# Token transposes of the last part: from TensorE passes to VectorE block transposes and on-chip transfers

## The chip, the cores and the metric

The kernel runs on one core of one Trainium2 chip. The metric is the device time of one execution in microseconds. Before the change three runs gave 5923.83 (the median), 5930.9 and 5917.58 us.

## What is computed

The input is x, 32 images of 128 channels by 64 x 64 pixels, f32. Cut to what matters:

```python
x = x + conv(group_norm(x), weight, butterfly matrices)   # in a transform domain, 64 x 64 per image
t = x.reshape(32, 128, 4096).transpose(0, 2, 1)           # tokens: 4096 x 128 per image
n = layer_norm(t)
k, v = n @ Wk.T + bk, n @ Wv.T + bv
probs = softmax(einsum('sbe,sbf->sef', k, v) / sqrt(32))
t = t + einsum('sef,sbf->sbe', probs, n)
n = layer_norm(t)
p = softmax(n @ router_w + router_b); the two best experts of 8, their p scaled to sum 1
t = t + sum over the two of p_e * (n @ expert_w[e] + expert_b[e])
out = t.transpose(0, 2, 1)
```

In the attention each image has its own 128 x 128 matrix of scores over channels; the sum runs over that image's 4096 tokens. The outer `x` after the convolution is called x1 below: it lies with channels on the 128 partitions, and attention and experts want tokens there.

## The kernel before

The kernel has three parts, one after the other. The first normalizes each image and transforms it (to about 940 us), the second multiplies by the convolution's weights for each of 64 columns (to about 2560 us). Both are untouched. The third part (`transfers`, `conv`, `front` and `experts`, from L800 on) takes image after image through these stages. An image has 32 tiles of 128 tokens, handled as 8 groups of four.

- `conv`: inverse transform by TensorE (`pu` L910, `py` L933; for images 0 and 1 in smaller pieces, `pw` L961 and `pz` L982), ScalarE copies between, and VectorE's sum with the image `y` (L942, op `ho`), which leaves x1 in a tile `x1_b` of 16 x 2 x 4 x 32 elements per partition.
- `front`, op `pt` (L1066): four TensorE transposes of 128 x 128 bring a group of x1 to tokens in PSUM. Op `to` (L1071): ScalarE copies the group into the token tile `tk` of this image (two tiles in turn, [128, 32, 128], so image b shares its tile with image b-2). Op `sa` (L1035, L1037): VectorE takes the statistics of four token tiles.
- then `pwa` and `na` (a power on ScalarE, a Newton step on GpSimd), `xg` (L1101, ScalarE: normalized tokens), `pg` (L1112, TensorE: Gram matrix), the small softmax chain (`gs`, `pb`, `t1`, `sm`, `pr`, `pc`, `prx`), `pp` (L1185, TensorE: x1 times the folded attention matrix and router), `at` (L1196, ScalarE), `ad` (L1211 to L1213 and statistics, VectorE: adds into `tk`), and the choice of experts (`l2` to `gt`, VectorE).
- `experts`: `xn` (L1300, ScalarE), `px` (L1310, TensorE transposes), `xT` (L1316, ScalarE), `pe` (L1323, TensorE: 64 products of 128 x 512 per image into three PSUM buffers), `m` (L1334, VectorE: product times gate, into `tm`), `s` (L1359 to L1362, GpSimd: sums over experts, into `tk`), `so` (L1368, VectorE: stream transposes of 32 x 32 blocks into `so`), `os` (L1378, SP: four stores per group).

What sets the order: every op is added to a `Plan` with engine, estimated time, due time, and the ops it comes after. The third part does not use the planner's own order. A table `ORDER`, written out by hand, lists all ops of one image with a stage (0 to 4); an op of image b stands at b + stage + its place in the table, and small shifts in `EDGE` move ops of images 0, 1, 30 and 31. `follow` issues them in that order, so each engine's queue is fixed: five images are in flight, and an engine that waits for one op holds all ops behind it. SP's queue holds the loads `r` (two per op) and `y` and the stores `os`. `room` counts buffers: 3 PSUM tiles for `pe`, 2 (`tl`) for `pt`, `px`, `pp` and the softmax chain, 8 rings for `r`, 4 `xg`, 2 each of `xn`, `tm`, `so`.

Of the kernel before, what the change touches and what calls it, by code (L numbers as in the profile page):

```python
# [10 lines left out]
F32 = mybir.dt.float32  # L11
# [92 lines left out]
def kernel(  # L104
# [732 lines left out]
    kvb = kc.tile([P, 2, P], F32, name="kvb")  # L837
    nc.gpsimd.dma_start(kvb[:, 0, :], bk.partition_broadcast(P))
    nc.gpsimd.dma_start(kvb[:, 1, :], bv.partition_broadcast(P))
    u = up.tile([P, n, P], F32, name="u")  # L840
    tk = [ct.tile([P, NT, P], F32, name=f"tk{i}") for i in range(2)]
    xg = [ct.tile([P, 4, P], F32, name=f"xg{i}") for i in range(NG)]
# [26 lines left out]
    plan = Plan({"cv": 1, "pe": 3, "tl": 2, "r": 8, "xg": NG, "xn": 2, "tm": 2, "so": 2})  # L869
# [157 lines left out]
    def front(b):  # L1027

        t = tk[b % 2]
        v = {}  # L1030

        def bn(which, lo, hi):
            bs = st.tile([P, 4, 6], F32, name=f"bs{which}_{b}_{lo}", tag="bs", bufs=2)
            for i in range(lo, hi):
                nc.vector.bn_stats(bs[:, i - lo, :], t[:, i, :])  # L1035
            for i in range(lo, hi):
                nc.vector.bn_aggr(v["mv", which][:, i, :], bs[:, i - lo, :])  # L1037
# [22 lines left out]
        def turn(g):  # L1060
            def run():
                ps = tile_of["pt", b, g] = tps.tile([P, 512], F32, tag="tl", name=f"pt{b}_{g}")
                x1 = ys[b].rearrange("c l v a w -> c (l v a w)")
                for k in range(4):
                    i = 4 * g + k
                    nc.tensor.transpose(ps[:, k * P : (k + 1) * P], x1[:, i * P : (i + 1) * P], ident)  # L1066
            return run

        def turned(g):
            def run():  # L1070
                nc.scalar.copy(  # L1071
                    t[:, 4 * g : 4 * g + 4, :].rearrange("p k c -> p (k c)"), tile_of.pop(("pt", b, g))
                )
            return run
# [10 lines left out]
        for g in range(8):  # L1085
            at = s1 + 0.016 * g
            add(b, f"pt{g}", "PE", 0.48, at, turn(g), [(b - 2, f"so{g}")] + [f"ho{k}" for k in range(4)], ("tl",))
            add(b, f"to{g}", "ACT", 0.55, at, turned(g), [f"pt{g}"], (), ("tl",))
            add(b, f"sa{g}", "DVE", 0.85, at, stats1(g), [f"to{g}"] + (["sa0"] if g else []))
# [6 lines left out]
        def norm(g):  # L1096
            def run():
                rstd, nmr, above = (v[1][:, k, :] for k in range(3))
                for k in range(4):
                    i = 4 * g + k  # L1100
                    nc.scalar.activation(  # L1101
                        xg[g % NG][:, k, :], t[:, i, :], AF.Identity, bias=above[:, i : i + 1], scale=rstd[:, i : i + 1]
                    )
            return run

        def gram(g):
            def run():
                if g == 0:
                    v["pg"] = tps.tile([P, 512], F32, tag="tl", name=f"pg{b}")
                for k in range(4):  # L1110
                    i = 4 * g + k
                    nc.tensor.matmul(  # L1112
                        v["pg"][:, 0:P], xg[g % NG][:, k, :], xg[g % NG][:, k, :],
# [4 lines left out]
        for g in range(8):  # L1118
            at = s1 + 0.26 + 0.016 * g
            add(b, f"xg{g}", "ACT", 1.65, at, norm(g), ["na", (b if g >= NG else b - 1, f"pg{(g - NG) % 8}")], ("xg",))  # L1120
# [85 lines left out]
        def added(lo, m):  # L1206
            def run():
# [3 lines left out]
                nc.vector.tensor_tensor(t[:, lo : lo + m, :], ps[:, :, 0:P], t[:, lo : lo + m, :], ALU.add)  # L1211
# [79 lines left out]
    def experts(b):  # L1291
        t = tk[b % 2]

        def normal(g):
            def run():
                rstd, nmr = tile_of["norm", b]
                x = tile_of["xn", b, g] = wp.tile([P, 4, P], F32, tag="xn", name=f"xn{b}_{g}")
                for k in range(4):
                    i = 4 * g + k
                    nc.scalar.activation(  # L1300
                        x[:, k, :], t[:, i, :], AF.Identity, bias=nmr[:, i : i + 1], scale=rstd[:, i : i + 1]
# [39 lines left out]
        def weighed(i, half):  # L1341

            def run():
                ps = tile_of.pop(("pe", b, i, half))
                for e in range(4):
                    nc.vector.scalar_tensor_tensor(  # L1346
                        t[:, i, :], ps[:, e * P : (e + 1) * P], tile_of["gate", b][:, i, 4 * half + e : 4 * half + e + 1],
                        t[:, i, :], ALU.mult, ALU.add,
# [6 lines left out]
        def summed(j):  # L1355
            def run():
# [4 lines left out]
                for m in range(2):  # L1361
                    nc.gpsimd.tensor_tensor(t[:, lo : lo + 2, :], t[:, lo : lo + 2, :], tm[:, :, m, :], ALU.add)  # L1362
            return run

        def flip(g):
            def run():
# [3 lines left out]
                    in_=t[:, 4 * g : 4 * g + 4, :].rearrange("p t (k c) -> p t k c", c=32),  # L1370
# [44 lines left out]
    for b in range(B):  # L1415
# [5 lines left out]
        s1:4 px2:4 m4_0:4 pe5_0:4 xT2:4 m5_1:4 pwa:3 pe6_0:4 ho0:2 px3:4 pe4_1:4 h1:2 m4_1:4 xn6:4 m5_0:4 na:3  # L1421
        m6_0:4 pe6_1:4 ho1:2 s2:4 xg0:3 pe7_1:4 pe7_0:4 m7_0:4 m6_1:4 h2:2 xT3:4 so0:4 xg2:3 xg1:3 m7_1:4 pe8_0:4
        ho2:2 pe9_0:4 s3:4 m8_0:4 xg3:3 pe8_1:4 m9_0:4 pg0:3 m8_1:4 pg1:3 pe9_1:4 xg5:3 pe10_1:4 pe10_0:4 m9_1:4
        xg4:3 pe11_0:4 s4:4 m10_0:4 pg2:3 so1:4 pg3:3 xg6:3 os1:4 xg7:3 pg4:3 pe11_1:4 xn5:4 pg5:3 m11_1:4 m11_0:4
        pg6:3 r1:1 m10_1:4 pg7:3 s5:4 pe12_0:4 gs:3 pe13_1:4 m12_0:4 pb:3 pe12_1:4 t1:3 pe13_0:4 os0:4 r2:0 pb2:3
        h3:2 sm:3 m13_0:4 pr:3 xT4:4 sr:3 m12_1:4 sn:3 m13_1:4 pe14_0:4 s6:4 m14_0:4 pc:3 pe15_1:4 pe15_0:4 prx:3
        ho3:2 pp0:3 m15_0:4 px5:4 at0:3 pe14_1:4 m15_1:4 pe19_0:4 m14_1:4 xT5:4 ad0:3 pe18_0:4 xn7:4 s7:4 pp6:3
        m18_0:4 pe19_1:4 at6:3 pp9:3 w0:1 m19_0:4 m19_1:4 at9:3 ad6:3 pe18_1:4 r7:1 wo0_0:1 ad9:3 pe16_0:4 wo0_1:1
        pp21:3 m18_1:4 pe16_1:4 at21:3 m16_0:4 so3:4 s9:4 pp12:3 m16_1:4 w1:1 at12:3 ad21:3 r4:0 x:1 os3:4 pe17_1:4
        wo1_0:1 ad12:3 pe17_0:4 wo1_1:1 pp24:3 m17_1:4 pe22_0:4 m17_0:4 at24:3 s8:4 pp3:3 m22_0:4 w2:1 at3:3 ad24:3  # L1430
        pe23_0:4 ad3:3 wo2_0:1 pe22_1:4 wo2_1:1 pp30:3 m22_1:4 pe23_1:4 m23_0:4 at30:3 pp15:3 m23_1:4 w3:1 ad30:3
        at15:3 s11:4 so4:4 pe21_1:4 ad15:3 wo3_0:1 r5:0 os4:4 px6:4 pe20_0:4 wo3_1:1 pe20_1:4 m20_0:4 xT6:4 pp18:3
        m20_1:4 pe21_0:4 m21_1:4 at18:3 pp27:3 m21_0:4 w4:1 at27:3 s10:4 ad18:3 pe26_0:4 ad27:3 wo4_0:1 pe27_1:4
        pe26_1:4 m26_0:4 pwb:3 m27_1:4 pt0:2 so2:4 pe24_0:4 m26_1:4 pe27_0:4 m24_0:4 pt1:2 m27_0:4 to0:2 nb:3
        pe25_1:4 to1:2 so5:4 wo4_1:1 pe25_0:4 m25_1:4 os5:4 s13:4 px7:4 m25_0:4 pe24_1:4 xT7:4 l2:3 xn0:3 pt2:2 f1:3
        w5:1 f2:3 pt5:2 pe30_0:4 m24_1:4 wo5_0:1 f3:3 pe31_0:4 wo5_1:1 s12:4 pe30_1:4 m30_0:4 to2:2 to5:2 w6:1 sa0:2
        m31_0:4 m30_1:4 pe31_1:4 pt4:2 m31_1:4 pt3:2 to4:2 f4:3 pe28_1:4 px0:3 pe29_1:4 sa5:2 wo6_0:1 s15:4 sa4:2
        wo6_1:1 sa1:2 pe28_0:4 w7:1 xn1:3 f5:3 xT0:3 to3:2 m28_0:4 so6:4 m28_1:4 m29_1:4 os6:4 pe29_0:4 xn4:3 pt6:2
        m29_0:4 px1:3 gt:3 pe0_0:3 s14:4 to6:2 pe1_1:3 m0_0:3 r6:0 os2:4 pe0_1:3 m1_1:3 wo7_0:1 pe1_0:3 pe3_0:3
        px4:3 wo7_1:1 sa6:2 m1_0:3 m0_1:3 pe2_0:3 xn3:3 xn2:3 xT1:3 sa2:2 s0:3 pe3_1:3 m2_0:3 h0:1 m3_1:3 so7:4  # L1440
        m3_0:3 sa3:2 os7:4 pe2_1:3 pt7:2 r0:0 r3:0 pe4_0:3 pe5_1:3 m2_1:3 to7:2 sa7:2
# [3 lines left out]
            at:-0.001152 f:0.024239 gs:-0.002876 gt:0.000645 h:-0.088197 ho:-0.107173 l:-0.011950 m:-0.001978  # L1445
            na:-0.062269 nb:0.023962 os:0.037831 pb:-0.003357 pc:0.004368 pe:-0.004859 pg:-0.007392
            prep:-0.061921 prx:-0.000723 pt:-0.339605 pwa:-0.154931 pwb:0.037324 px:0.004889 r:-0.551854
            s:-0.000175 sa:-0.148905 sm:-0.006267 sn:0.000807 so:-0.001240 sr:0.003296 t:-0.002368 to:-0.321139
            w:-0.120521 wo:-0.109642 x:0.001867 xT:0.001275 xg:0.001692 xn:0.024691
        """,  # L1450
        1: """
            ad:0.003202 at:0.005763 f:0.005458 gs:-0.006322 gt:-0.000499 h:0.054990 ho:0.051746 l:-0.039944
            m:-0.001956 na:-0.011054 nb:-0.006237 os:0.010755 pc:-0.007414 pe:-0.000758 pg:0.001613 pr:-0.004399
            prx:-0.010090 pt:-0.015523 pwa:0.002034 pwb:0.001095 px:-0.002083 r:0.003449 s:-0.001956 sa:0.014227
            sn:-0.012403 so:-0.008148 sr:-0.010178 t:0.008140 to:0.002048 w:-0.000799 wo:-0.000193 xT:-0.009151
            xg:0.001343 xn:0.009969
        """,
        B - 2: """
            ad:-0.000137 at:0.005214 f:0.009800 gt:0.013838 h:-0.001798 ho:-0.002170 l:0.001614 m:0.011670
            na:0.002329 nb:-0.000549 os:0.199427 pb:-0.000148 pc:-0.004225 pe:0.008786 pg:-0.022172 pp:-0.005288  # L1460
            pr:-0.000058 prx:-0.004077 pt:-0.004342 pwa:-0.000635 pwb:-0.005281 px:0.016961 r:-0.007120
            s:0.049524 sa:-0.000213 sm:0.000159 sn:0.010880 so:0.176068 sr:0.012703 t:0.003951 w:0.001356
            wo:-0.009915 x:0.098978 xT:0.012789 xg:0.005833 xn:0.039799
        """,
        B - 1: """
            ad:0.016785 at:0.025250 f:0.011554 gt:0.005035 h:0.014633 ho:-0.003864 m:0.001746 na:0.022282
            nb:0.003897 os:0.161384 pb:-0.000741 pc:-0.008894 pe:0.004175 pg:0.007134 pp:0.006191 pr:-0.001474
# [75 lines left out]
```

## Time and profile before

| | |
|---|---|
| profiled execution | 5924.1 us, span of the core 5922.4 us |
| granted TensorE clock, mean | 0.993 |
| busy of the span: TensorE, VectorE, ScalarE, GpSimd | 98%, 72%, 65%, 67% |
| third part begins, first expert product | about 2560 us, 2679.4 us |
| `pt`, TensorE, in 3500 to 5500 us | 612 rows, mean 273 ns |
| `to`, ScalarE copy of 128x512 | 153 rows, mean 584 ns |
| `so`, VectorE stream transpose of 128x512 | 156 rows, mean 704 ns |
| stores `os` on SP, 64 KB | 1024, median 434 ns of SP each |
| loads `r` on SP, 256 KB | 496, median 589 ns of SP each |
| DMA | 756.88 MB, mean 128 GB/s |

How to read it: a busy row is the union of an engine's instructions. TensorE's instructions overlap, so the mean of a matmul row is longer than its share of the queue. Rows named SPq are times in which SP issued a transfer, not the transfer. In a line of groups the numbers behind the bar are busy us and mean ns of one, and behind the second bar the idle time just before, with what ended it. Some matmul rows are missing from the record (612 of about 628 here).

### The profile page before, as it was taken

What the parts mean: (1) busy time and instruction counts of PE and PEld (TensorE: products, weight loads), DVE (VectorE), ACT (ScalarE), POOL (GpSimd) and SP (SyncE); (2) the same over time, 40 slices, a digit from 0 to 9 for tenths busy, and PEclk for the clock granted to TensorE, in tenths of its full rate; (3) what the DMA queues carried; (4) which work ended last, traced back from release to release, by engine and by line L of the source; (5) the groups of instructions that cost most, each with busy time, mean ns of one, the idle gap of its engine ahead of it and who ended that gap; (6) DMA issues with size and microseconds to landing.
All of it is one profiled execution on the core that took longest, in us unless ns stands there. A gap on an engine that the chain in (4) does not pass through costs nothing. (4 is left out here: it accounts for less than half of the span.)

```text
span 5922.4 us, 221064 instructions
## 1 busy us (share of the span) xinstructions
PE 5789.1 (98%) x94348; PEld 4560.4 (77%) x94348; DVE 4235.4 (72%) x10353; ACT 3837.7 (65%) x7089; POOL 3947.6 (67%) x4210
## 2 busy tenths in 40 slices
PE   7999999999999999979999999999999999999997
PEld 7999999999999999976666666666666666666653
DVE  5565555555555555538888878788888888787877
ACT  7666664555555555557777777777777777777762
POOL 2110006666666666607888888888888888888887
PEclk9999999999999999989999999999999999999999
DMA  5767766666666666652323222233223222222201
GB/s 194 241 228 233 236 210 206 171 174 171 171 173 173 172 172 173 158 159 61 97 76 87 79 79 87 82 88 83 88 75 97 76 84 81 79 86 83 77 21 29
DMA packets 664681, 756.88 MB, mean 128 GB/s; under 512 B 70608, under 2 KB 462288, under 8 KB 659600
## 3 DMA queue, kind: packets, MB, share of 16 engines
q1 hardware_dynamic: 661088, 733.69, 43.0%
q8 instruction: 740, 12.12, 0.9%
q0 software_dynamic: 2608, 9.06, 0.5%
q14 instruction: 245, 2.01, 0.1%
HBM read 406.79 MB, written 335.54 MB: 125 GB/s over the span
## 5 line engine op out<-in xcount | busy, mean ns | idle before, releaser
L1323 PE MATMUL pe<-ew_sb,xT 128*128 128x512 f32 x4096 | 1973.2, 600 | 36.6 <-DVE tm L1334 22.8
L1334 DVE TENSOR_TENSOR tm<-pe,oh 128x512 f32<-128x512 f32 x2028 | 1298.4, 678 | 369.1 <-PE pe L1323 259.4
L1359 POOL TENSOR_TENSOR tm<-tm 128x512 f32<-128x512 f32 x1014 | 1270.4, 1272 | 287.0 <-DVE tm L1334 282.2
L1323 PEld LDWEIGHTS pe<-ew_sb,xT 128*128 128x128 f32 x4096 | 691.8, 190 | 552.1 <-issue 325.3
L660 DVE COPY f<-g 128x1024 f32<-128x1024 f32 x508 | 622.4, 1225 | 651.9 <-PE g L649 651.9
L671 PE MATMUL m<-f,s 128*64 128x64 f32 x32768 | 1071.3, 224 | 1.7 <-ACT f L660 0.8
L671 PEld LDWEIGHTS m<-f,s 128*64 128x64 f32 x32768 | 1001.1, 138 | 63.2 <-issue 2.5
L617 POOL COPY s<-l 128x512 f32<-128x512 f32 x512 | 546.2, 1102 | 527.3 <-issue 510.4
L660 ACT COPY f<-g 128x1024 f32<-128x1024 f32 x508 | 514.9, 1014 | 562.4 <-PE g L649 536.3
L1362 POOL TENSOR_TENSOR tk<-tk,tm 128x256 f32<-128x256 f32 x1014 | 737.9, 728 | 79.5
L1360 POOL TENSOR_TENSOR tm<-tm 128x512 f32<-128x512 f32 x507 | 644.7, 1272 | 39.8
L649 PE MATMUL g<-c,wst 9*128 9x128 f32 x16256 | 601.2, 284 | 4.5 <-issue 4.1
L921 ACT COPY u<-pu 64x512 f32<-64x512 f32 x960 | 558.0, 581 | 67.8 <-PE pu L910 58.7
L1196 ACT ACTIVATE pp<-pp,ln 128x128 f32<-128x128 f32 x1024 | 442.3, 432 | 230.9 <-PE pp L1185 157.2
L649 PEld LDWEIGHTS g<-c,wst 9*128 9x128 f32 x16256 | 504.0, 187 | 39.5 <-issue 4.8
L619 POOL TENSOR_SCALAR s<-l 128x512 f32<-128x512 f32 x256 | 509.6, 1991 | 0.0
L362 POOL TENSOR_TENSOR grstd<-gms,mhalf 128x1 f32<-128x1 f32 x32 | 17.7, 554 | 736.4 <-DVE gms L358 736.4
L431 PE MATMUL pf<-ph,v 128*128 128x128 f32 x4096 | 491.2, 278 | 5.5 <-ACT z L396 1.1
L910 PEld LDWEIGHTS pu<-qw,r 128*128 128x128 f32 x3840 | 456.8, 193 | 34.0 <-ACT u L921 22.2
L431 PEld LDWEIGHTS pf<-ph,v 128*128 128x128 f32 x4096 | 466.9, 192 | 15.5 <-ACT z L396 7.2
L910 PE MATMUL pu<-qw,r 128*128 128x128 f32 x3840 | 471.2, 276 | 4.9 <-ACT u L921 4.8
L1035 DVE BATCH_NORM_STATS2 bs<-tk 128x6 f32<-128x128 f32 x2048 | 449.5, 280 | 24.5 <-ACT tk L1071 23.2
(176 smaller groups left out, 7978.4 us busy)
## 6 DMA issues: line engine op xcount, KB each, us to landing
xf<-f SPq DMA_DIRECT2D x512, 256.0 KB
pf<-o SPq DMA_DIRECT2D x1016, 128.0 KB
l<-xf SPq DMA_DIRECT2D x1012, 128.0 KB
r<-pf SPq DMA_DIRECT2D x496, 256.0 KB
x<-in_x_dram SPq DMA_DIRECT2D x256, 256.0 KB
out_dram<-so SPq DMA_DIRECT2D x1024, 64.0 KB
y<-in_x_dram SPq DMA_DIRECT2D x31, 2048.0 KB
r<-pf POOLq DMA_DIRECT2D x16, 248.0 KB, 8.3
```

The lines of the kernel that those rows point to most:

```text
L431: nc.tensor.matmul(pl[:, j * P : (j + 1) * P], vs[b][:, 8 * g + j, :], ph.rearrange("h r m -> h (r m)"), start=True, stop=True,)
L617: nc.gpsimd.tensor_copy(dst, src)
L649: nc.tensor.matmul(pg[g // 2][:, g % 2, m * P : (m + 1) * P], wst[rows, 16 * half + 4 * t + m, :], c[rows].rearrange("r h k -> r (h k)"), ...
L660: copy(f.rearrange("i m (g o) -> i m g o", g=2), tile_of["g", w, half, t][k].rearrange("i g (o m) -> i m g o", o=4))
L671: nc.tensor.matmul(ps[hh * n : (hh + 1) * n, q, :], s[:, h].rearrange("i k b -> i (k b)")[:, B * r : B * r + n], f[:, h, r, :], start=(r = ...
L910: nc.tensor.matmul(ps[:, k, :], rs[b, e][:, k * P : (k + 1) * P], qw.rearrange("w r m -> w (r m)"), start=True, stop=True,)
L921: nc.scalar.copy(u[r * n : (r + 1) * n, :, oh * n + 8 * e : oh * n + 8 * e + 8], ps[oh * n : (oh + 1) * n, :, r * n : (r + 1) * n].rearran ...
L1323: nc.tensor.matmul(ps, tile_of["xT", b, i // 4][:, i % 4, :], ew_sb[:, es, :].rearrange("d e c -> d (e c)"), start=True, stop=True,)
L1334: nc.vector.tensor_tensor(tile_of["tm", b, i // 2][:, i % 2, es, :], tile_of.pop(("pe", b, i, half)).rearrange("p (e c) -> p e c", c=P), t ...
L1359: nc.gpsimd.tensor_tensor(tm[:, k, 0:4, :], tm[:, k, 0:4, :], tm[:, k, 4:8, :], ALU.add)
L1360: nc.gpsimd.tensor_tensor(tm[:, :, 0:2, :], tm[:, :, 0:2, :], tm[:, :, 2:4, :], ALU.add)
L1362: nc.gpsimd.tensor_tensor(t[:, lo : lo + 2, :], t[:, lo : lo + 2, :], tm[:, :, m, :], ALU.add)
```

## The change

The ops `pt` and `to` are replaced. Op `tr` (VectorE, eight per image) transposes a group of x1 in 32 x 32 blocks into half of a staging tile `tt` (two buffers of [128, 4, 8, 32]). Op `td` (SP, four per image) then sends 16 transfers of 32 partitions by 1 KB each from `tt` to `tk`, which puts the blocks on the right partitions: block (channel group k, column group a) goes to partitions 32a and to piece k of the token tile. `tk` becomes [128, 4, 32, 32]: four channel groups, then token tile, then 32 channels, and all readers use the view `tokens`, in which a token's 128 channels are four pieces of 32. Two of the four `xg` tiles now lie in `ebb` and the attention biases in another of them, so `xg` of image 0 comes after `prep`. `ORDER` and `EDGE` are written anew; in the new table `w` to `ho` of an image stand about a third of a period earlier against the rest.

```diff
-    kvb = kc.tile([P, 2, P], F32, name="kvb")
...
-    tk = [ct.tile([P, NT, P], F32, name=f"tk{i}") for i in range(2)]
-    xg = [ct.tile([P, 4, P], F32, name=f"xg{i}") for i in range(NG)]
+    tk = [ct.tile([P, 4, NT, 32], F32, name=f"tk{i}") for i in range(2)]
+    tokens = [t.rearrange("p k i c -> p i k c") for t in tk]
+    xg = [ebb[:, 0:4, :], ebb[:, 4:8, :]] + [ct.tile([P, 4, P], F32, name=f"xg{i}") for i in range(2, NG)]
+    kvb = xg[NG - 1][:, 0:2, :]
...
         def turn(g):
             def run():
-                ps = tile_of["pt", b, g] = tps.tile([P, 512], F32, tag="tl", name=f"pt{b}_{g}")
-                x1 = ys[b].rearrange("c l v a w -> c (l v a w)")
+                if g % 2 == 0:
+                    tile_of["tt", b, g // 2] = wp.tile([P, 4, 8, 32], F32, tag="tt", name=f"tt{b}_{g}")
+                x1 = ys[b].rearrange("c l v a w -> c (l v) a w")
+                nc.vector.transpose(
+                    out=tile_of["tt", b, g // 2][:, :, 4 * (g % 2) : 4 * (g % 2) + 4, :].rearrange("p a i c -> p i a c"),
+                    in_=x1[:, 4 * g : 4 * g + 4],
+                )
+            return run
+
+        def moved(c):
+            def run():
+                tt = tile_of.pop(("tt", b, c))
                 for k in range(4):
-                    i = 4 * g + k
-                    nc.tensor.transpose(ps[:, k * P : (k + 1) * P], x1[:, i * P : (i + 1) * P], ident)
-            return run
-
-        def turned(g):
-            def run():
-                nc.scalar.copy(
-                    t[:, 4 * g : 4 * g + 4, :].rearrange("p k c -> p (k c)"), tile_of.pop(("pt", b, g))
-                )
+                    for a in range(4):
+                        nc.sync.dma_start(
+                            tk[b % 2][32 * a : 32 * a + 32, k, 8 * c : 8 * c + 8, :].rearrange("p i c -> p (i c)"),
+                            tt[32 * k : 32 * k + 32, a].rearrange("p i c -> p (i c)"),
+                        )
             return run
...
-            add(b, f"pt{g}", "PE", 0.48, at, turn(g), [(b - 2, f"so{g}")] + [f"ho{k}" for k in range(4)], ("tl",))
-            add(b, f"to{g}", "ACT", 0.55, at, turned(g), [f"pt{g}"], (), ("tl",))
-            add(b, f"sa{g}", "DVE", 0.85, at, stats1(g), [f"to{g}"] + (["sa0"] if g else []))
+            add(b, f"tr{g}", "DVE", 0.7, at, turn(g), [f"ho{k}" for k in range(4)] + ([f"tr{g - 1}"] if g % 2 else []), ("tt",) if g % 2 == 0 else ())
+            if g % 2:
+                add(b, f"td{g // 2}", "SP", 6.4, at, moved(g // 2), [f"tr{g - 1}", f"tr{g}", (b - 2, f"so{g - 1}"), (b - 2, f"so{g}")], (), ("tt",), 3.0)
+        for g in range(8):
+            at = s1 + 0.016 * g
+            add(b, f"sa{g}", "DVE", 0.85, at, stats1(g), [f"td{g // 2}"] + (["sa0"] if g else []))
...
-                nc.vector.tensor_tensor(t[:, lo : lo + m, :], ps[:, :, 0:P], t[:, lo : lo + m, :], ALU.add)
+                nc.vector.tensor_tensor(
+                    t[:, lo : lo + m], ps[:, :, 0:P].rearrange("p k (a c) -> p k a c", c=32), t[:, lo : lo + m], ALU.add
+                )
...
-                    nc.gpsimd.tensor_tensor(t[:, lo : lo + 2, :], t[:, lo : lo + 2, :], tm[:, :, m, :], ALU.add)
+                    part = tm[:, :, m, :].rearrange("p i (a c) -> p i a c", c=32)
+                    nc.gpsimd.tensor_tensor(t[:, lo : lo + 2], t[:, lo : lo + 2], part, ALU.add)
```

The queue of SP per image in the built program of the change, in order: `r7 r0 os0 r6 td0 r4 os1 r2 r5 td1 os3 os2 r1 r3 y os5 td2 os4 td3 os6 os7`.

## The prediction

> **What bounds the kernel now.** I read the row of 40 slices first: TensorE is at 9 from slice 18 on, at full clock. So I asked for the busy time in 100 us stretches of the last part (the columns are the five engines' busy time, then granted clock, DMA share and rate):
>
> ```profile
> core 0: us, PE busy (x) PEld busy (x) DVE busy (x) ACT busy (x) POOL busy (x), PEclk, DMA share, GB/s
> ...
> 4000.00:4100.00 100.00, 99.82 (x705) 67.24 (x704) 83.95 (x261) 73.78 (x166) 85.37 (x95) 1.00 0.30 85
> 5600.00:5700.00 100.00, 97.51 (x663) 62.38 (x662) 83.71 (x263) 68.12 (x156) 85.72 (x93) 1.00 0.08 22
> 5700.00:5800.00 100.00, 86.56 (x329) 46.60 (x327) 81.22 (x270) 57.43 (x138) 87.04 (x97) 0.98 0.07 19
> ```
>
> A busy matmul row alone proves little, because matmuls overlap, so I asked next what TensorE waits for between 3000 and 5500 us. The whole answer is one line:
>
> ```profile
> PE pe L1323 <- DVE tm L1334: 0.3, 1, 0.3
> ```
>
> TensorE never waits there: it is the bound. Its period comes from the chain of work in order of time, where one `py` piece recurs once per image:
>
> ```profile
> 4316.52 2.02 PE py L933 x64
> ...
> 4418.36 2.02 PE py L933 x64
> ...
> 4520.20 2.02 PE py L933 x64
> ```
>
> 101.84 us, twice. The saturated stretch runs from the first expert product (2679.4) to the end of the last `py` piece (5674.41 + 2.02 = 5676.4): 2997 us, 29.4 periods. The rest of the span is 2679 us before it and 246 us after it, where VectorE and GpSimd share the limit (93% and 91% in the last 125 us).
>
> **What is removed.** Eight groups of four `pt` transposes per image. Their cost on a saturated queue is the distance to the next start, not the 273 ns of a row, so I read TensorE's own timeline:
>
> ```profile
> 4092.70 0.60 PE L1066 MATMUL pt<-ident,x 128*128 128x128 f32 x4
> 4093.14 2.74 PE L1323 MATMUL pe<-ew_sb,xT 128*128 128x512 f32 x6
> ...
> 4098.36 1.04 PE L1066 MATMUL pt<-ident,x 128*128 128x128 f32 x8
> 4099.23 1.02 PE L1323 MATMUL pe<-ew_sb,xT 128*128 128x512 f32 x2
> ```
>
> 0.44 us for four, 0.87 for eight: 8 x 0.435 = 3.48 us per image. The period can fall to 98.36 us; 29.4 x 3.48 = 102 us. ScalarE loses eight copies of 0.584 us (4.7 us per image). It has 26% idle, so I value that at nothing; nothing waits for it once the copies' own readers are gone.
>
> **What is added on VectorE.** Eight 32x32 stream transposes of 128x512 per image. The trace has the same instruction with the same shape, and the groups of the stretch 3500 to 5500 price it, beside what else reads the new layout:
>
> ```profile
> L1362 POOL TENSOR_TENSOR tk<-tk,tm 128x256 f32<-128x256 f32 x628 | 457.1, 728 | 49.2
> ...
> L1368 DVE STREAM_TRANSPOSE so<-tk 128x512 f32<-128x512 f32 x156 | 109.8, 704 | 1.2 <-DMA r<-pf 0.4 <-POOL tm L1359 0.4
> ...
> L1066 PE MATMUL pt<-ident,x 128*128 128x128 f32 x612 | 88.7, 273 | 0.0
> L1071 ACT COPY tk<-pt 128x512 f32<-128x512 f32 x153 | 87.3, 584 | 122.3 <-PE pt L1066 113.0 <-POOL ln L1051 8.3 <-POOL ln L1050 0.6
> ```
>
> 8 x 0.704 = 5.6 us. VectorE now has 0.8395 x 101.84 = 85.5 us per image; 91.1 of 98.36 is 93%. Of its present idle time, the waits that are not for expert products (for POOL, for `sm`, `gs`, `t`; 112.6 us in 19.6 images) are 5.7 us per image. 91.1 + 5.7 = 96.8, so only 1.5 us per image remain for new waits before VectorE paces the loop.
>
> Here the Trainium skill speaks against the change. "VectorE: DVE Perf Modes", section Rules for kernel authors, sends a 128x128 transpose to TensorE when PSUM will do, and VectorE's transposes stay inside 32x32 blocks (section The three transpose paths). By engine time the rule is right: the rows say 0.435 us on TensorE plus 0.584 on ScalarE against 0.704 on VectorE plus 8 transfers. Followed as a rule it leaves the 3.48 us where they are. I go by the waits instead: TensorE's time is the only time here that the end pays for.
>
> **Tokens in four pieces of 32.** Every reader of `tk` (`xg`, `xn`, statistics, `ad`, POOL's sums, `so`) now takes four runs of 128 bytes that lie 4 KB apart. No row has that step. Near ones: POOL's butterfly products (L234) take 316 to 323 ns at nearly every run length from 32 down to 1 element, and `so` already reads blocks of 32. I take zero. Unknown side: the first POOL row above would have to grow by 0.35 us (32 per image) before POOL (87.1 us per image now) reaches 98.36. I exclude a gain, since the same elements are read.
>
> **What is added on SP.** 64 transfers of 32 KB per image, in four batches of 16. Prices: SP spends 0.434 us on a store of 64 KB and 0.472 us on the only transfer between SBUF tiles in the trace (`r<-o`, 8 KB). 64 x 0.45 = 29 us; SP's present 32 stores, 16 `r` halves and `y` make 14 + 9 + 0.5 = 24. 53 of 98 us: room. The 16 DMA engines have room too: 661088 packets of the hardware queue took 43.0% of their span, 62 ns each, so 2048 more packets of 1 KB per image are 8 us on 16 engines, beside a share of 0.30. Here is a second rule: "DMA: Bandwidth & Descriptors", Rules for kernel authors, says that under 64 KB one pays mostly overhead, and the section Anatomy of one DMA puts a fixed 2.0 us on each (there for the GpSimd path). Paid one after another, that is 64 x 2.0 = 128 us per image, SP would need over 150 and the kernel would take about 5924 + 29.4 x 50 = 7400 us. The row says otherwise, for four stores go out in 1.8 us:
>
> ```profile
> 4002.70 1.76 SPq L1378 DMA_DIRECT2D out_dram<-so  x4
> ```
>
> I use the row, and the fixed time only once, as the landing of a batch. But the built program lets at most eight of SP's transfers be in flight: each waits for the one eight before it.
>
> **The new wait.** The built order shows two tight batches. `td0` waits for `so1` and is needed by `sa0`; `td3` waits for `so7` and is needed by `sa7`. A batch takes 16 x 0.472 = 7.6 us plus a landing. For `r<-o`, SP's last issue ends at 2551.8 and TensorE, waiting for it, goes on at 2553.9: 2.1 us. Together 9.7. On VectorE between `so1` and `sa0` stand seven expert products (0.62 each back to back), two transposes and the softmax pieces, 6.7 us, plus their usual waits (55.1 us in 20 images = 2.8): 9.4. Between `so7` and `sa7`: eight products, one x1 sum, three statistics groups: 5.0 + 1.2 + 3.7 = 9.9. So both are in time to within 0.3 us. If one is late, queued behind it on VectorE are the next expert products; TensorE goes on for its three PSUM buffers, 3 x 0.86 = 2.6 us. Bounds: none lost, or the whole lateness. I take 0.5 us per image, 15 us. `td1` and `td2` have over 15 us each. Stores `os0` to `os7` stand behind batches by up to 8 us; their two buffers are next needed later than that. `r` and `y` loads move too, but the next images' use is a large part of a period away.
>
> **The ends.** Image 0 has no neighbour to hide its batches. Before, its last statistics end at 2593.0. After: x1 is complete at 2573.4, plus 1.4 (two transposes), 64 x 0.434 = 27.8, the 13 loads queued between (7), landing 2.1, last statistics 1.2: 2613. The longer path meets fewer of image 1's ScalarE copies, so I carry 12 of these 20 us on; 4 us of `py` work is then already done before the first expert product. Net +8 (0 to 25). In the tail image 31's x1 is ready a third of a period earlier in the order, but VectorE carries its transposes and `sa7` waits for `td3`: +5 (-10 to 20).
>
> **Sum**, against the profiled execution's 5924.1 us (span 5922.4; the runs' median is 5923.8): 5924.1 - 102 + 15 + 8 + 5 = 5850 us.
>
> **Rivals.**
> (a) VectorE paces the loop. For: only 1.5 us of margin, with waits in a fixed order. Period 99.8 instead of 98.9: 29.4 x 0.9 = 26 us more, 5876 (to 5912 at 101). Against: its waits for TensorE (163 us in 19.6 images) shrink first.
> (b) The batches are late, and the kernel is slower. Place: `sa0` and `sa7`. Price: if a small transfer lands as late as the `r` load on the chain (5.35 us), the ninth of a batch must wait 2.0 us for the first, and the last lands at 15.0 us instead of 9.7. Both uses are then 5.3 us late, 10.6 less twice a cushion of 2 is 6.6 us per image against 3.48 saved: 29.4 x 3.1 = 92, with the ends about 6030. It decides from a batch of about 13 us on. Against: the room on the DMA engines above.
> (c) Ends cost nothing and no wait shows: 5815.
>
> **Chances.** Forecast 0.55 (5825 to 5870); (a) 0.22; (b) 0.15; (c) 0.05; gain and new waits cancelling 0.03. The measurement tells about 0.2% (12 us) from no change. Faster 0.81, same 0.04, slower 0.15. For 8 in 10 the range reaches from just above (c) through (a): 5818 to 5915.
>
> **What would show it.** Right: `py` recurs every 98.4 to 99 us; TensorE's waits stay under 1 us per image; stream transposes stay near 0.70; POOL's sums into `tk` stay near 728 ns; VectorE waits for `tk` transfers at `sa0` and `sa7` for under 1 us each. Wrong: a period of 101.8 or more with VectorE idle before statistics (b), TensorE waiting for `tm` with VectorE at 97% (a), or longer POOL and ScalarE rows (layout).

## The result

The change made the kernel slower: 6001.6 us (median of four runs, 5998.9 to 6008.4) against 5927.4 us for the kernel before (four runs, 5917.6 to 5933.1), a ratio of 1.0132 with a 95% interval of 1.012 to 1.0144. The forecast was 5850 us with a range of 5818 to 5915: the time moved the other way and lies outside the range.

The profiled execution took 6001.4 us (span 5999.7). The table cuts both spans at two marks: the end of the last `so` of image 0 and of image 29.

| | before | after | difference | forecast |
|---|---|---|---|---|
| start to last `so` of image 0 | 2790.2 | 2827.3 | +37.1 | +8 |
| from there to last `so` of image 29 (29 periods) | 2953.3 | 2995.3 | +42.0 | -86 |
| from there to the end | 178.9 | 177.1 | -1.8 | +5 |

So the tail was right, the front cost 29 us more than said, and the loop missed by 128 us: 103.28 us per image, where 98.36 + 0.5 was forecast. The granted TensorE clock is 1.00 from 2830 to 5700 us in both profiles, so the clock is no part of the loop's loss.

### The profile page after: what moved, and what is told of

Its sections match the earlier page's. It is cut to its first block, busy times and chain, and to the rows that moved or that the text cites. A ratio compares the mean times of both kernels' runs of the same rounds, so it can differ in the third digit from the quotient of the medians.

```text
span 5999.7 us, 222547 instructions
## 1 busy us (share of the span) xinstructions
PE 5749.2 (96%) x93324; PEld 4455.2 (74%) x93324; DVE 4371.4 (73%) x10609; ACT 3684.9 (61%) x6833; POOL 3938.4 (66%) x4210
```

## The profile after

First what held. The groups of the stretch 3500 to 5500 us show that the layout in four pieces costs nothing and that a stream transpose costs what `so` costs (the columns are busy us and mean ns of one, then idle time before):

```profile
L1375 POOL TENSOR_TENSOR tk<-tk,tm 128x256 f32<-128x256 f32 x620 | 449.6, 725 | 48.6
...
L1066 DVE STREAM_TRANSPOSE tt<-x 128x512 f32<-128x512 f32 x154 | 105.9, 697 | 18.4 <-DMA tk<-tt 11.8 <-DMA out_dram<-so 5.0 <-issue 1.6
L1381 DVE STREAM_TRANSPOSE so<-tk 128x512 f32<-128x512 f32 x154 | 102.9, 686 | 0.0
```

Before, the GpSimd sum took 728 ns and `so` 704, and 704 was the price set for the new transpose: the forecast holds.

What failed is the period. One `py` piece of each image, from TensorE's timeline:

```profile
4067.22 2.09 PE L934 MATMUL py<-hm,u 128*64 128x64 f32 x64
...
4169.25 2.09 PE L934 MATMUL py<-hm,u 128*64 128x64 f32 x64
...
4274.19 2.08 PE L934 MATMUL py<-hm,u 128*64 128x64 f32 x64
```

102.03 us, then 104.94: longer than the 101.84 of before, and no longer even. A period that wanders suggests that something unsteady, such as a transfer, sets it. VectorE's waits between 3500 and 5500 us (us in total, times, longest; 19.4 images) name one:

```profile
DVE tm L1346 <- PE pe L1335: 70.6, 96, 1.6
DVE bs L1036 <- DMA tk<-tt: 54.8, 36, 2.4
...
DVE tt L1066 <- DMA tk<-tt: 11.8, 12, 1.9
```

54.8 + 11.8 us, with 9.5 us more that the trace books on `out_dram<-so` for the same instructions, are 3.9 us per image of new waits for transfers: 3.1 before statistics (`bs`), and 0.9 before transposes that need a staging tile (`tt`) that an earlier batch has not yet emptied, a wait that the forecast did not list. The time that VectorE still waits for TensorE's products fell from 163.3 us to 70.6. SP's timeline of one period gives the batches behind these waits, the first row being `td3`, the third `td0`:

```profile
4068.56 10.01 SPq L1077 DMA_DIRECT2D tk<-tt  x16
4078.62 5.46 SPq L1391 DMA_DIRECT2D out_dram<-so  x8
...
4094.74 10.04 SPq L1077 DMA_DIRECT2D tk<-tt  x16
```

A batch takes 10.0 us of SP at the least, up to 11.7 in other periods, not 7.6: 0.63 us per transfer. VectorE's own timeline shows both readers waiting:

```profile
4080.18 0.87 DVE L1036 BATCH_NORM_STATS2 bs<-tk 128x6 f32<-128x128 f32 x4 [1.52 <-DMA tk<-tt]
...
4106.14 0.87 DVE L1036 BATCH_NORM_STATS2 bs<-tk 128x6 f32<-128x128 f32 x4 [0.85 <-DMA tk<-tt]
```

The landing adds 1.6 and 1.4 us, so a batch is over after 11.5 us. The windows that VectorE's other work left were as forecast or longer (4078.66 - 4068.5 = 10.2 us and 4105.3 - 4094.6 = 10.7, against 9.9 and 9.4); the batch was longer still.

But four us of VectorE waits are only dear if VectorE is what TensorE waits for, and in the forecast it was not. Here is one period of the kernel before in five stretches of 20 us from the last `so` of an image on, where the prediction read one stretch of 100 us (the columns are busy us of PE, PEld, DVE, ACT, POOL):

```profile
core 0: us, PE busy (x) PEld busy (x) DVE busy (x) ACT busy (x) POOL busy (x), PEclk, DMA share, GB/s
4012.40:4032.40 20.00, 20.00 (x208) 12.62 (x203) 14.86 (x35) 14.63 (x33) 18.63 (x24) 1.00 0.27 67
4032.40:4052.40 20.00, 20.00 (x154) 13.85 (x153) 10.93 (x21) 8.95 (x25) 17.20 (x18) 1.00 0.30 81
4052.40:4072.40 20.00, 20.00 (x113) 14.68 (x112) 19.50 (x82) 18.27 (x43) 15.68 (x15) 1.00 0.41 133
4072.40:4092.40 20.00, 19.96 (x108) 13.47 (x107) 19.10 (x60) 16.30 (x34) 15.87 (x20) 1.00 0.29 91
4092.40:4112.40 20.00, 19.86 (x95) 12.19 (x93) 19.56 (x77) 16.41 (x36) 18.05 (x19) 1.00 0.20 54
```

VectorE's 84% is 64% in the first 40 us of a period and 97% in the last 60, and seven of the eight `pt` groups lie in the last 30 of those 60. There TensorE was busy with VectorE full beside it, not with VectorE at rest. The waits of the weight loads say so too (rows PEld; us in total, times, longest, 3500 to 5500 us). The weight loads, unlike the matmuls, did wait for VectorE before the change, and after it they waited almost three times as long:

```profile
PEld pe L1323 <- DVE tm L1334: 51.7, 138, 1.0
```

```profile
PEld pe L1335 <- DVE tm L1346: 144.7, 355, 1.2
```

After the change the same five stretches are

```profile
4068.50:4088.50 20.00, 19.80 (x114) 12.35 (x111) 17.45 (x59) 12.78 (x24) 17.64 (x24) 1.00 0.31 82
4088.50:4108.50 20.00, 19.58 (x102) 13.12 (x101) 12.38 (x33) 16.16 (x41) 19.06 (x20) 1.00 0.41 110
4108.50:4128.50 20.00, 19.29 (x111) 13.87 (x110) 19.57 (x81) 17.49 (x41) 14.46 (x14) 1.00 0.38 97
4128.50:4148.50 20.00, 19.28 (x91) 12.16 (x90) 18.98 (x71) 15.76 (x34) 14.63 (x21) 1.00 0.62 188
4148.50:4168.50 20.00, 19.79 (x232) 11.76 (x231) 19.55 (x38) 8.71 (x23) 19.06 (x19) 1.00 0.20 54
```

again 60 us with VectorE at 95 to 98%, and TensorE is no longer full in any of the five.

The front: image 0's batches on SP, and the first expert product on TensorE, which before came at 2679.4 us.

```profile
2577.57 13.84 SPq L1077 DMA_DIRECT2D tk<-tt  x16
...
2594.64 15.94 SPq L1077 DMA_DIRECT2D tk<-tt  x16
...
2616.66 24.47 SPq L1077 DMA_DIRECT2D tk<-tt  x32
```

```profile
2715.72 1.02 PE L1335 MATMUL pe<-ew_sb,xT 128*128 128x512 f32 x2
```

The batches meet the `r` loads of image 1 and take 12 to 16 us each, one after the other; between 2577 and 2641 us SP waits 7.8 us for `r` loads and 4.2 us for the load `y` to land. Image 0's last statistics end at 2644.8 instead of 2593.0, 52 us later, and the first product comes 36 us later. TensorE's granted clock from 2560 to 2720 us was 0.82, against 0.90 before; how much of the 36 us that is, the runs do not show.

## The experiments

"Period" is the distance of the last `so` of image 0 from that of image 29, divided by 29. Each ratio is to the kernel before as it ran beside that run; its median was 5919.5 us beside e9 and e10 and 5924.2 to 5927.4 beside the others, so compare runs of different groups by their ratios.

| run | time, us | ratio, 95% interval | first product, us | period, us |
|---|---|---|---|---|
| before | 5927 | | 2679.4 | 101.84 |
| after | 6001.6 | 1.0132, 1.012 to 1.0144 | 2715.7 | 103.28 |
| e2 no transposes | 5956.7 | 1.0052, 1.0037 to 1.0067 | 2712.0 | 101.82 |
| e3 neither | 5864.5 | 0.9899, 0.9882 to 0.9916 | 2688.3 | 99.49 |
| e4 half of the transfers | 5889.0 | 0.9938, 0.9923 to 0.9952 | 2697.7 | 100.23 |
| e5 before without `pt`, `to` | 5906.8 | 0.9971, 0.996 to 0.9982 | 2674.5 | 101.21 |
| e6 readers moved | 6078.7 | 1.0264, 1.0247 to 1.0281 | 2712.0 | 105.81 |
| e7 same, image 0 by TensorE | 6051.8 | 1.0217, 1.0202 to 1.0232 | 2688.0 | 105.83 |
| e9 two queues | 5948.1 | 1.0051, 1.0036 to 1.0066 | 2706.5 | 101.74 |
| e10 same, image 0 by TensorE | 5922.6 | 1.0009, 1.0 to 1.0019 | 2683.1 | 101.58 |
| e11 same, chain first | 5913.7 | 0.9979, 0.997 to 0.9988 | 2691.1 | 101.14 |
| e12 before, extra in the slack | 5928.1 | 1.0004, 0.9995 to 1.0013 | 2678.9 | 101.81 |
| e13 before, extra in the full part | 5981.9 | 1.0092, 1.0078 to 1.0106 | 2683.1 | 103.53 |

### Take the change apart: e2, e3, e4

Theory L is that the batches land late and that TensorE loses what VectorE loses by it. Rival V is that VectorE's load with its eight transposes, or the new order by itself, paces the loop. e2 leaves the transposes out and sends two constant staging tiles:

```diff
-                nc.vector.transpose(
-                    out=tile_of["tt", b, g // 2][:, :, 4 * (g % 2) : 4 * (g % 2) + 4, :].rearrange("p a i c -> p i a c"),
-                    in_=x1[:, 4 * g : 4 * g + 4],
-                )
```

> The changed kernel without VectorE's eight stream transposes per image: the transfers are all made, from two constant staging tiles, and the statistics wait for them (x1 never reaches the tokens; this part is left out). Theory L: the two tight batches start at so1 and so7 as before and take 11 to 12 us with landing, so the period stays at 102 to 103 us, time 5950 to 5990. Rival V: VectorE has 5.6 us per image less to do, the period falls to about 99, time 5860 to 5890.

Measured 5956.7 us, period 101.82: close to theory L's 102, far from V's 99. With 5.6 us per image less on VectorE, 2.33 us of the period (101.82 - 99.49, the run without both) still go to the batches. Its VectorE waits for them as much as after the change (us in 19.6 images):

```profile
DVE bs L1040 <- DMA tk<-tt: 61.1, 37, 2.6
```

e3 leaves out the transfers as well:

```diff
-                        nc.sync.dma_start(
-                            tk[b % 2][32 * a : 32 * a + 32, k, 8 * c : 8 * c + 8, :].rearrange("p i c -> p (i c)"),
-                            tt[32 * k : 32 * k + 32, a].rearrange("p i c -> p (i c)"),
-                        )
```

> The changed kernel with neither the transposes nor the transfers (x1 never reaches the tokens; this part is left out), in the changed order: what the loop would take if the new path cost nothing. Both theories: period 98.4 us, the front back to about 2680, time 5800 to 5825. If it stays above 5850, the new order itself costs time, whatever the path does.

Measured 5864.5 us, period 99.49: neither theory's 98.36. Even with the new path for nothing, 1.13 us of the 3.48 that the passes took on TensorE do not come back. TensorE's own waits in this run, 7.2 us for `xT` and 6.2 for `tm` in 20.1 images against 0.3 in all before, are 0.67 us per image of it; the rest is not traced.

e4 sends 8 of 16 transfers:

```diff
-                for k in range(4):
+                for k in range(2):
                     for a in range(4):
```

> The changed kernel with only 8 of the 16 transfers of each batch (two of the four channel groups never reach the tokens; this part is left out); all waits stay. Theory L: a batch takes 8 x 0.633 + about 0.6 + 1.1 for the landing = 6.8 us, within the 9.4 and 9.9 us that VectorE leaves, so the period falls to 98.4 to 99.5 us; image 0's four batches shrink by about 30 us; time 5840 to 5870. Rival V: the load of VectorE is unchanged, period 102 or more, 5940 to 5960.

Measured 5889.0 us, period 100.23: 19 us above L's upper end, but 51 us below V's lower. Statistics wait for transfers no more (4.2 us in 20 images), with all transposes in place. The 0.74 us over e3 are what the transposes and batches that are in time cost; the 3.05 us up to 103.28 come with the other half of the transfers, that is, by VectorE's waits, with the lateness. The split depends on the order of taking apart: by e2 the batches cost 2.33 us and the transposes 1.46 (103.28 - 101.82). Either way the batches are the larger part. Of VectorE's 3.9 us of waits, 2.3 to 3.05 came through to the end.

### What the passes were worth: e5

```diff
-                for k in range(4):
-                    i = 4 * g + k
-                    nc.tensor.transpose(ps[:, k * P : (k + 1) * P], x1[:, i * P : (i + 1) * P], ident)
...
-                nc.scalar.copy(
-                    t[:, 4 * g : 4 * g + 4, :].rearrange("p k c -> p (k c)"), tile_of.pop(("pt", b, g))
-                )
```

> The kernel before without its token transposes on TensorE and their copies on ScalarE (x1 never reaches the tokens; this part is left out): the most that taking these passes off TensorE can bring in the old order. By the prediction's own price (8 x 0.435 us per image) the period falls from 101.84 to 98.36 us and the time to 5815 to 5830. Rival: other waits come up as soon as TensorE is relieved (in the changed order without transposes and transfers the period was 99.49 us), period 99.2 or more, time above 5840.

Measured 5906.8 us, period 101.21: the rival, and more so than it was put. In the old order the passes can be left out altogether for 0.63 us per image, not 3.48. The last two of its five stretches of 20 us show why, beside the 19.96 and 19.86 of TensorE before:

```profile
4059.90:4079.90 20.00, 19.62 (x97) 12.44 (x96) 19.13 (x60) 15.70 (x32) 16.02 (x21) 1.00 0.24 67
4079.90:4099.90 20.00, 18.38 (x80) 9.90 (x81) 19.59 (x77) 13.86 (x31) 18.20 (x19) 1.00 0.21 53
```

VectorE is as full as ever; TensorE has less to do and waits for it, where before it waited 0.3 us (19.8 images):

```profile
PE pe L1320 <- DVE tm L1331: 38.1, 97, 0.7
```

These are 1.9 of the 2.85 us per image that do not come back.

### Is it the stretch, or the mean? e12, e13

Both are the kernel before with four more stream transposes per image, 2.8 us, of constant data into a scratch tile; they differ only in the place. `DU` names the expert products behind which they stand in e12; in e13 these are `m20_1`, `m26_0`, `m24_0` and `m30_0`.

```diff
+        for g in range(4):
+            add(b, f"du{g}", "DVE", 0.7, s1, lambda: nc.vector.transpose(out=scr, in_=ew_sb[:, 0:4, :].rearrange("p e c -> p (e c)")))
...
+    DU = ['m7_1', 'm8_0', 'm9_0', 'm10_0']
```

> The kernel before with four more stream transposes of 128x512 per image on VectorE (constant data into a scratch tile, 2.8 us), placed in the first 40 us of the period, where VectorE is busy 14.9 and 10.9 of 20 us. Theory P (what counts is the stretch, not the mean of the period): no change, period 101.8 to 102.0, time within 0.2% of before. If VectorE's mean load of 84% counted, an eighth of the addition or more would show, but the same in both places.

> The same four transposes placed in the last 60 us of the period, where VectorE is busy 19.5, 19.1 and 19.6 of 20 us although its mean is 84%. Theory P: VectorE paces TensorE there already, so 1 to 2.8 us per image come through: period 102.8 to 104.6, time 30 to 80 us over before. If the mean load counted, as the prediction took it, TensorE's queue would go on at 101.84 and nothing would show.

Measured 1.0004 (0.9995 to 1.0013) and 1.0092 (1.0078 to 1.0106). The same instructions cost nothing in the first 40 us (they start 14 to 22 us after the last `so`) and 1.69 us per image in the last 60 (66 to 86 us after it). In e12 they come mostly out of VectorE's waits for products (163.3 us before), in e13 TensorE's weight loads wait for VectorE twice as long as before (51.7 us):

```profile
DVE tm L1337 <- PE pe L1326: 126.5, 128, 2.0
```

```profile
PEld pe L1326 <- DVE tm L1337: 99.2, 215, 1.3
```

This bears theory P out directly: the mean load of the period does not tell what an addition costs.

### The price of one transfer: e8

Behind the last store of the kernel before, 16 transfers each between the token tiles, by kind; the first kind is shown.

```diff
+    for j in range(16):
+        nc.sync.dma_start(d[32 * (j // 4) : 32 * (j // 4) + 32, 256 * j : 256 * j + 256], s[32 * (j % 4) : 32 * (j % 4) + 32, 256 * j : 256 * j + 256])
...
```

> The kernel before with 128 small transfers between the two token tiles behind its last store, 16 of a kind, to measure one transfer's price on its queue: 32 partitions by 1 KB (the kind of the changed kernel), by 2 KB, by 512 bytes, 128 partitions by 256 bytes, 512 bytes, 1 KB, all from SP; then 32 by 1 KB from ScalarE's queue, and from both in turn. Theory: the price goes by the transfer and not by its bytes, 0.63 us each for every kind, and two queues in turn halve it. Rival: it goes by bytes or rows, 0.45 us or less for 512 bytes, over 1 us for 2 KB; or one generator serves both queues, and two in turn give 0.63 us each as well. The run's time only tells that the tail was added, about 80 to 120 us more than before.

The one execution took 5993 us. SP's timeline, in the order 32 rows of 1 KB, of 2 KB, of 512 bytes, 128 rows of 256 bytes, of 512 bytes, of 1 KB; ahead of them 16 of the stores to DRAM:

```profile
5919.98 10.10 SPq L1492 DMA_DIRECT2D tk<-tk  x16
5930.14 10.08 SPq L1494 DMA_DIRECT2D tk<-tk  x16
5940.26 10.29 SPq L1496 DMA_DIRECT2D tk<-tk  x16
5950.60 10.24 SPq L1498 DMA_DIRECT2D tk<-tk  x16
5960.89 10.25 SPq L1500 DMA_DIRECT2D tk<-tk  x16
5971.18 10.52 SPq L1502 DMA_DIRECT2D tk<-tk  x16
```

0.63 to 0.66 us each for 16 to 128 KB: the price goes by the transfer. A row of the first kind takes 540 ns, so the pace of 0.63 us is longer than the row. And from both queues in turn (ns of one, least, median and most, then first and last start):

```profile
L1506 SPq DMA_DIRECT2D tk<-tk x8: 540/547/581, 5981.8 to 5986.3; - x8
L1506 ACTq DMA_DIRECT2D tk<-tk x8: 601/602/607, 5984.0 to 5988.5; - x8
```

ScalarE's eight take the same 0.6 us each while SP's eight are still going out: two queues issue side by side. The Trainium skill ("DMA: Bandwidth & Descriptors", Rules for kernel authors) says that spreading transfers over issuing engines brings no bandwidth and only saves issue time. The saving is what this trace shows, and issue time is what lacks here; the bandwidth no run here tested.

### Repairs: e6, e7, e9, e10, e11

e6 moves readers of the tight batches, and what hangs on them, in the table (`sa6` and `sa7` go to the next image's pass, hence stage 3); here is one of the lines that change:

```diff
-        s2:4 m6_0:4 pwa:3 m7_1:4 tr0:2 so0:4 m7_0:4 w2:1 pe8_0:4 pe6_1:4 na:3 m8_0:4 pe8_1:4
...
+        s2:4 m6_0:4 m7_1:4 tr0:2 so0:4 m7_0:4 sa7:3 sa6:3 pwa:3 w2:1 pe8_0:4 pe6_1:4 m8_0:4 pe8_1:4 na:3
...
```

> The changed kernel, complete, with eight entries of its order moved so that the readers of the tight batches come later on VectorE: the first two statistics groups about two expert products later, the last two (and the power, the Newton step and the first normalized group behind them) about five later, and two transposes that waited for a staging buffer. Theory L (late batches): the waits for transfers vanish and the period falls from 103.3 to 100.2 us, where it was with half the transfers; the front keeps its loss; time 5905 to 5925. Rival V (VectorE's load): period stays above 102.5, time 5975 or more. A third outcome, period 101 to 102.5, would say that moving the readers only moves the wait to the softmax chain behind them.

Measured 6078.7 us, period 105.81. By its numbers this is V's outcome, but the waits point elsewhere than to VectorE's load. The statistics' waits for transfers are gone; GpSimd's Newton step now stands in its queue ahead of sums and waits for the later statistics (0.2 us after the change),

```profile
POOL ln L1049 <- DVE mv L1038: 59.4, 19, 3.9
```

and VectorE in turn waits for GpSimd's sums for 115 us (44.1 after the change):

```profile
DVE tm L1346 <- POOL tk L1375: 115.0, 31, 5.8
```

It also took the statistics out of the gaps of the softmax chain, where VectorE now waits with nothing to do (`prx` for `pc`, 21 us). Which of these waits makes how much of the 2.5 us per image was not taken apart.

e7 adds `pt` and `to` for image 0, e10 does the same in e9:

```diff
+            if b == 0:
+                add(b, f"pt{g}", "PE", 0.48, at, turn_first(g), [f"ho{k}" for k in range(4)], ("tl",))
+                add(b, f"to{g}", "ACT", 0.55, at, turned_first(g), [f"pt{g}"], (), ("tl",))
+                continue
...
```

> As the run with moved readers, and image 0 alone gets its tokens in the old way, by TensorE transposes and ScalarE copies (31 images by transfers). If the loss at the front is image 0's four batches in a row, the first expert product comes at about 2690 us instead of 2715 and the time is 20 to 28 us under that run's, 5880 to 5900. If it is the new order of the front, nothing changes.

Measured 26.9 us under e6, first product at 2688.0 instead of 2712.0: as expected for the front, though not the 5880 to 5900, since e6 itself had missed. Image 0's last statistics end 55 us earlier (2586.0 instead of 2641.1), of which 24 arrive at the first product. So of the change's 36 us at the front, 24 to 27 go with image 0's batches (27 by e3, whose first product comes at 2688.3), and about 9 stay with the new order without them.

e9 shortens the fourth batch (SP sends 10, ScalarE 6), puts `m14_1` ahead of `sa0` and `tr4` behind `m24_0`:

```diff
+        add(b, "ta3", "ACT", 3.8, s1, moved(3, 10, 16, nc.scalar), ["tr6", "tr7", (b - 2, "so6"), (b - 2, "so7")])
...
-        pe4_0:3 m4_0:3 xn3:3 wo0_0:0
+        pe4_0:3 m4_0:3 xn3:3 ta3:2 wo0_0:0
...
```

> The changed kernel, complete, with the last tight batch shortened instead of its readers moved: 6 of the 16 transfers of the fourth batch go out on ScalarE's queue, just before the image's first copy out of the inverse transform, where ScalarE waits about 10 us anyway; and one expert product is put ahead of the first statistics group, one transpose four products later. Theory L: the fourth batch takes 10 x 0.633 + 0.6 + 1.1 = 8.0 us, inside the 9.9 us before its readers; the waits of VectorE for transfers fall from about 4 us per image to under 1 and the period from 103.3 to 100.3 to 101.3 us; time 5915 to 5945. Rival: the readers' lateness was only a cover for other waits, as where the readers were moved; period 102.3 or more, time 5975 or more.

Measured 5948.1 us, period 101.74: by the ratios 0.8% (some 48 us) better than the change, 3 us above the expected time and between the two expected periods. The waits fell as said, from 3.9 us to 0.9 per image, one an image, at the first group:

```profile
DVE bs L1036 <- DMA tk<-tt: 17.6, 19, 1.9
```

But that group stands within the softmax chain, and its wait comes out again on TensorE (16.0 us after the change; no such wait in e3 and e4, where the statistics are in time):

```profile
PE pc L1173 <- ACT pr L1169: 22.6, 19, 2.2
```

> The same, and image 0 gets its tokens in the old way, by TensorE transposes and ScalarE copies. As with the moved readers this takes 24 to 27 us off the front; time 5890 to 5920, which would be 0.1 to 0.6% below the kernel before.

Measured 5922.6 us, ratio 1.0009 (1.0 to 1.0019): 25.6 us better than e9, as expected for the front, but not below the kernel before.

e11 moves two entries of the table:

```diff
-        sa0:2 pr:3 pe15_1:4 px5:4 pe17_1:4 sr:3 sn:3 sa1:2 pc:3 xT5:4 pe16_0:4 xn7:4 prx:3 m15_1:4 pp0:3
+        pr:3 pe15_1:4 px5:4 pe17_1:4 sr:3 sa0:2 sn:3 pc:3 xT5:4 pe16_0:4 xn7:4 prx:3 sa1:2 m15_1:4 pp0:3
```

> As the run with two queues and image 0 by TensorE, with the first two statistics groups taken out of the softmax chain: they stand behind the reciprocal and behind the copy of the folded matrix now. There TensorE waited for the transposed probabilities, 1.1 us per image. Theory L: this wait was the late batch handed on through VectorE's fixed order; period 101.6 falls to 100.5 to 100.8, time 5890 to 5905, below the kernel before by 0.3 to 0.5%. Rival: VectorE works at its limit from there on anyway, so the later statistics push the same time into the stretch behind; period stays at 101.3 or more, time 5915 to 5925.

Measured 5913.7 us, ratio 0.9979 (0.997 to 0.9988), period 101.14: between the two. The wait on `pc` is gone, but only 0.44 of its 1.1 us stay gained. TensorE's waits for `tm` rose from 12.7 us in e10 to

```profile
PE pe L1358 <- DVE tm L1369: 20.0, 62, 0.6
```

which is 0.37 us per image, so much of the rest came back as the rival had it, in the stretch behind. The first product also came 8.0 us later than in e10. This is the best version found with the new path, 0.2% under the kernel before and 1.5% under the change. Its period is still 1.65 us over that of e3. Four of its eight transposes start within 28 us of the last `so`, the other four at 41, 73, 79 and 96 us, in VectorE's full stretch.

## Why the prediction was wrong

Against 98.36 us, the 103.28 are made up so: 1.13 that do not come back (e3), 0.74 for the transposes and the batches as far as they are in time (e4 - e3), 3.05 for late batches (after - e4). The forecast had 0, 0 and 0.5. The largest miss is the late batches, 2.5 us per image or 74 us in 29 periods (by e2's split 1.8 us). With the batches in time, if only at half of the transfers (e4), the kernel is 38 us faster than before.

1. "TensorE never waits there: it is the bound." This is the step that failed first. It was read from TensorE's busy row and the waits of its matmuls, not of its weight loads, with VectorE's mean over 100 us. In 60 of these 100 us VectorE was at 97% and TensorE had little room to gain (e5: 0.63 us instead of 3.48; e12 and e13: the same work free in one place and 1.69 us in the other). In the new order, which puts the work otherwise, 2.35 of 3.48 came back.
2. "8 x 0.704 = 5.6 us. VectorE now has 85.5 us per image; 91.1 of 98.36 is 93%." The durations were right, the sum against the mean was not. Rival (a) names this mechanism, but as a margin of the whole period; priced by stretches it would have stood first.
3. "A batch takes 16 x 0.472 = 7.6 us plus a landing." The term was mis-sized: 0.472 came from a transfer of 8 KB among other work, 0.434 from a store. And 0.472 is the length of a row, where the pace counts: the new rows of 589 ns follow each other at 0.63 us. A transfer between SBUF tiles costs SP 0.63 to 0.66 us for 16 to 128 KB (e8), 10.0 us the batch and up to 11.7. The 0.5 us set for lateness rested on margins of 0.3 us and on the cushion of the next point. The landing, 1.4 to 1.6 us, was smaller than the 2.1 that I took.
4. "TensorE goes on for its three PSUM buffers" and "it decides from a batch of about 13 us on": with VectorE at 95 to 98% behind, no cushion of 2 us shows. A batch of 11.5 us was enough, and both tight batches paid. Rival (b) was the mechanism on the side of the loss, at the place named, with the point of decision put too far out. e9 shows it from the other side: 3 us of waits taken away gave 1.54 us of period, with its two moved entries in the sum.
5. The front: +8 forecast, +36 measured. I laid 64 x 0.434 = 27.8 us on SP; the four batches took 14, 16 and 24 (two) us, 54 in all, of which 40 are the pace of 0.63 and 12 waits for image 1's `r` and `y` loads to land. So the delay of the last statistics was mis-sized: 52 us instead of 20. The share carried on was not the fault: 12 of 20 was assumed, 36 of 52 measured, and in e7 24 of 55.
6. A slip in the sums: rival (c), with no waits and no costs at the ends, is 5924 - 102 = 5822 us, not 5815; the measured time lies far from either.
7. Right: layout at no cost, transposes at 0.70, the fourth and first batch as the tight ones, SP with room on the whole, the tail.

The rule of "VectorE: DVE Perf Modes" (Rules for kernel authors) that sends a 128x128 transpose to TensorE fits this result better than my argument against it. My reason for setting it aside was that only TensorE's time counts; e5 shows that in this order TensorE's passes took 3.48 us of its queue and only 0.63 us of the period.

What stays open: whether a wholly new order could reach the 99.5 us of e3 with the transfers made. By e12 and e13 one would look to have all transposes in VectorE's first 40 us, which may need more than two staging tiles; no run has that.

## What to carry to other kernels

Before you call an engine the bound of a repeating loop, cut one period into stretches and read every engine in each: an engine at 84% can be at 97% in just the part that you change, and then little of what you take off another engine there comes back (0.63 of 3.48 us here), and most of what you add is paid (1.69 of 2.8). Count small transfers by number and not by bytes, from rows of the same kind (SBUF to SBUF, to DRAM), and by their distance, not their length. In a fixed order, moving the reader of a late transfer can put the wait elsewhere (e6 lost 2.5 us per image, e11 gained 0.44 of 1.1); here it paid more to shorten what is late, over a second queue at a moment when that engine idles (e9, 1.54).

## What the hardware showed

A transfer between SBUF tiles costs its queue 0.63 to 0.66 us from 16 to 128 KB, with 32 or with 128 rows, against 0.44 for a store of 64 KB to DRAM (1.76 us for four in the kernel before); in this range size is free, number is not. SP and ScalarE issue such transfers at that pace side by side (e8). Of the 2048 issues of the new transfers the median took 589 ns, but 71 took over 800, up to 2007: about every second batch has one such. What holds them, the runs do not show.
